# A sequential graph layer on one core: the recurrence in program order, its prepared work as tasks in the gaps

## The chip, the core and the metric

The kernel runs on one core of a Trainium2 chip. A core has TensorE (PE: matrix products, with a separate weight load, PEld), VectorE (DVE), ScalarE (ACT), GpSimd (POOL) and SyncE (SP, which here only issues DMA transfers). PE writes its products to PSUM, from which DVE and ACT read; the other data lie in SBUF. Time is the device time of one execution in microseconds; the time before is the median of 3 runs.

## The reference, cut to what matters

Four graph layers over 16 samples of 1024 nodes with 256 features, each of the form x = x + layer(relu(layernorm(x)), adj), all in float32. Layers 0 (attention), 1 (normalised adjacency) and 3 (two-layer network on neighbour sums) treat all nodes at once. Layer 2 is sequential: node i reads the new values of the nodes before it and the old values of the others.

```python
norm_adjT = jnp.swapaxes(adj, 1, 2) * dinv[:, :, None]

def step(h, i):
    x = jnp.take(h_e, i, axis=1)
    row = jnp.take(norm_adjT, i, axis=1)
    x_par = jnp.einsum('bj,bjd->bd', row, h)
    iou = x @ W_ioux.T + b_ioux + x_par @ W_iouh.T + b_iouh
    r, z = jnp.split(iou, 2, axis=1)
    r, z = (jax.nn.sigmoid(r), jax.nn.sigmoid(z))
    hc = jnp.tanh(x @ W_coux.T + b_coux + x_par * r @ W_couh.T + b_couh)
    h_new = z * x_par + (1.0 - z) * hc
    h = jax.lax.dynamic_update_slice(h, h_new[:, None, :], (0, i, 0))
    return (h, None)
h_out, _ = jax.lax.scan(step, h_e, jnp.arange(n))
```

## The kernel before

`layers_0_1()`, `layer_2()` and `layer_3()` run one after the other. In layer 2 the 1024 nodes are cut into 8 blocks of 128 (index t), and each block into 8 sub-blocks of 16 nodes (index s). 16 samples times 16 nodes make 256 rows, held as two groups (g) of 128 rows. The neighbour sum of a node has these parts:

- **base**: all blocks other than the one just before, with old or finished values; prepared one block ahead, as tasks (`base_tasks`);
- **last block**: the block just before; done between two blocks (`last_block`);
- **far** and **near**: sub-blocks of the same block that are done; near serves the next sub-block at once, far the later ones (`far_tasks`);
- inside the sub-block itself: the rounds. Three rounds (K = 3) always run. Each takes the change of h from the round before, spreads it over the adjacency inside the sub-block (`change`), and brings the gates up to date (`round_`). Where the chain of dependent nodes in a sub-block has more than three links, further rounds run (`one_more`), under a branch on a value that the kernel worked out from the data.

```python
def last_block(t, bxt, dv):
    for b0 in range(0, B, 4):
        hr = big.tile([P, 4, D], F32, name="hr")
        nc.sync.dma_start(hr, hn_d[b0 : b0 + 4, (t - 1) * P : t * P].rearrange("b p d -> p b d"))
        ao = big.tile([P, 4, P], F32, name="ao")
        nc.sync.dma_start(ao, a["adj"][b0 : b0 + 4, (t - 1) * P : t * P, t * P : (t + 1) * P] ...)
        nc.gpsimd.tensor_tensor(ao, ao, dv[:, b0 : b0 + 4], ALU.mult)
        for b in range(4):
            pb = psum.tile([P, DC, P], F32, name="pb")
            for c in range(DC):
                nc.tensor.matmul(pb[:, c], hr[:, b, c * P : (c + 1) * P], ao[:, b], start=True, stop=True)
            nc.vector.tensor_add(bxt[:, :, b0 + b], bxt[:, :, b0 + b], pb)

# gate_tasks(he, s): r (two tasks) and z with c (two tasks) of the inputs of sub-block s,
# wx products into PSUM tiles "pf", moved to gr (ACT) and gz (DVE)

def change(dh, x, ai):
    px = psum.tile([P, DC, G2 * GR], F32, name="px")
    ...                                     # px = dh x ai: 4 products of 128 columns
    for g in range(G2):
        add(pxr[:, g], aig[g], dh[:, g])    # the same sum with rows and columns swapped, kept in PSUM
    dx = work.tile([P, DC, G2 * GR], F32, name="dx", bufs=1)
    nc.vector.tensor_copy(dx[:, 0], px[:, 0])
    nc.scalar.activation(dx[:, 1], px[:, 1], AF.Copy)
    for c in range(DC):
        nc.vector.tensor_add(x[:, c], x[:, c], px[:, c])
    return dx

def round_(dx, x, rx, h, fill, to):
    ...                                     # pr += wh x dx: 4 products of 256 columns
    for e in range(DC):
        nc.scalar.activation(r[:, e], pr[:, e], AF.Sigmoid)
        nc.vector.tensor_mul(r[:, e], r[:, e], x[:, e])
        if rx is not None:
            nc.vector.tensor_sub(drx[:, e], r[:, e], rx[:, e])
    ...                                     # pz += dx x wh: 4 products of 256 columns
    nc.scalar.activation(z, pz, AF.Sigmoid)
    nc.scalar.activation(w, pz, AF.Sigmoid, scale=-1.0)
    fill()
    ...                                     # pc += drx x wh: 4 products of 256 columns
    nc.vector.tensor_mul(z, z, pxr)
    if h is not None:
        nc.vector.tensor_sub(z, z, h)
    fill()
    for g in range(G2):
        nc.scalar.activation(hc[:, g], pc[:, g], AF.Tanh)
        nc.vector.tensor_mul(w[:, g], w[:, g], hc[:, g])
        nc.vector.tensor_add(to[:, g], z[:, g], w[:, g])
    return r
```

The main loop, cut. The framework orders the instructions of each engine by itself, from the program and its own estimate of when each can start; `fill()` only says where in the program a share of the tasks stands.

```python
for t in range(NT):
    ...                                     # loads and base_tasks of block t + 1
    for s in range(NS):
        x = ...                             # bxt + near
        seed(x, *gx)                        # gates of the inputs into pr, pz, pc; x transposed into pxr
        ...                                 # gate_tasks of the next sub-block join the others
        fill()
        rx = round_(x, x, None, None, fill, ho)
        for k in range(1, K):
            dx = change(dh, x, ai)
            fill()
            ...                             # round_ again, with fill
        with tc.If(n_more[0][s] > 0, preferred_fallthrough_block=False):
            one_more(x, rx, h, ho, ai)      # no fill inside
            with tc.If(n_more[1][s] > 0, preferred_fallthrough_block=False):
                with tc.For_i(0, n_more[1][s], 1):
                    one_more(x, rx, h, ho, ai)
        for g in range(G2):
            nc.sync.dma_start(hn_d[g * GB : (g + 1) * GB, j0 : j0 + S], h[:, g])
        ...                                 # near products, far_tasks
    if t + 1 < NT:
        last_block(t + 1, bxt_next, dv_next)
```

Of the kernel before, what the change touches and what calls it, by code (L numbers as in the profile page):

```python
# [16 lines left out]
P = 128  # L17
# [9 lines left out]
K = 3  # L27
# [11 lines left out]
def gnn_stack(ctx: ExitStack, tc: tile.TileContext, a: dict, out: bass.AP):  # L39
# [273 lines left out]

    def layer_2():
        with ExitStack() as st:
# [28 lines left out]
            def levels():  # L344

                with ExitStack() as once:
# [14 lines left out]
                    pt = psum.tile([P, 2 * D], F32, name="pf", bufs=2)  # L361
# [16 lines left out]
            def base_tasks(t, bxt, dv):  # L378
# [4 lines left out]
                def load(b):  # L383
                    ab = big.tile([P, NT, P], F32, name="ab")
                    nc.sync.dma_start(ab, rows(a["adj"][b])[:, :, t * P : (t + 1) * P])
                    nc.gpsimd.affine_select(out=ab[:, t], in_=ab[:, t], compare_op=ALU.is_ge, fill=0.0, base=0,
                                            pattern=[[-1, P]], channel_multiplier=1)
                    hb = big.tile([P, NT, D], F32, name="hb")
                    if t > 1:
                        nc.sync.dma_start(hb[:, : t - 1], rows(hn_d[b])[:, : t - 1])  # L390
                    nc.sync.dma_start(hb[:, t:], rows(he_d[b])[:, t:])
                    loaded[b] = ab, hb

                def task(b, k, held):
                    def run():
                        if k == 0:
                            if b == 0:
                                load(0)
                            if b + 1 < B:
                                load(b + 1)  # L400
                            held.append(psum.tile([P, DC, P], F32, name="pb"))
# [3 lines left out]
                        for c, j in todo:  # L405
                            nc.tensor.matmul(pb[:, c], hb[:, j, c * P : (c + 1) * P], ab[:, j],  # L406
                                             start=j == jts[0], stop=j == jts[-1])
                        if k == len(jts) - 1:
                            nc.vector.tensor_mul(bxt[:, :, b], pb, dv[:, b][:, None].to_broadcast([P, DC, P]))
                            del loaded[b]  # L410
                    return run
# [8 lines left out]
            def last_block(t, bxt, dv):  # L420

                for b0 in range(0, B, 4):
                    hr = big.tile([P, 4, D], F32, name="hr")
                    nc.sync.dma_start(hr, hn_d[b0 : b0 + 4, (t - 1) * P : t * P].rearrange("b p d -> p b d"))
                    ao = big.tile([P, 4, P], F32, name="ao")
                    nc.sync.dma_start(ao, a["adj"][b0 : b0 + 4, (t - 1) * P : t * P, t * P : (t + 1) * P]
                                      .rearrange("b p i -> p b i"))
                    nc.gpsimd.tensor_tensor(ao, ao, dv[:, b0 : b0 + 4], ALU.mult)
                    for b in range(4):
                        pb = psum.tile([P, DC, P], F32, name="pb")  # L430
                        for c in range(DC):
                            nc.tensor.matmul(pb[:, c], hr[:, b, c * P : (c + 1) * P], ao[:, b], start=True, stop=True)
                        nc.vector.tensor_add(bxt[:, :, b0 + b], bxt[:, :, b0 + b], pb)

            def load_block(t):
# [7 lines left out]
                dp = big.tile([P, G2, P], F32, name="dp")  # L443
                for g in range(G2):
                    nc.sync.dma_start(dp[:, g], dinv_d[g * GB : (g + 1) * GB, t * P : (t + 1) * P][:, None]
                                      .to_broadcast([GB, S, P]))
                return he, dv, dp

            def load_sub(t, s, dp):


                j0 = t * P + s * S
                rem = P - s * S
                aj = big.tile([P, G2, P], F32, name="aj")
                for g in range(G2):
                    nc.sync.dma_start(aj[:, g, :rem], bass.AP(
                        tensor=a["adj"].tensor, offset=a["adj"].offset + g * GB * N * N + j0 * N + j0,
                        ap=[[N * N, GB], [N, S], [1, rem]]))
                nc.gpsimd.tensor_tensor(aj[:, :, :rem], aj[:, :, :rem], dp[:, :, s * S :], ALU.mult)
                ai = big.tile([P, G2, GB, S], F32, name="ai")  # L460
                for g in range(G2):
                    nc.gpsimd.tensor_tensor(ai[:, g], aj[:, g, :S][:, None].to_broadcast([P, GB, S]), before, ALU.mult)
                bd = None
                if s < NS - 1:
                    bd = big.tile([P, G2, GB, P - S], F32, name="bd")
                    for g in range(G2):
                        nc.gpsimd.tensor_tensor(
                            bd[:, g, :, : rem - S], aj[:, g, S:rem][:, None].to_broadcast([P, GB, rem - S]),
                            own[:, :, None].to_broadcast([P, GB, rem - S]), ALU.mult)
                return ai, bd  # L470

            def gate_tasks(he, s):


                hs = big.tile([P, DC, G2 * GR], F32, name="hs")
                for c in range(DC):
                    nc.gpsimd.tensor_copy(hs[:, c].rearrange("p (b i) -> p b i", b=B), he[:, c, :, s * S : (s + 1) * S])
                gr = big.tile([P, DC, G2 * GR], F32, name="gr")
                gz = big.tile([P, G2, 2 * D], F32, name="gz")

                def task_r(e):
                    def run():
                        pg = psum.tile([P, 2 * D], F32, name="pf", bufs=2)
                        for c in range(DC):
                            nc.tensor.matmul(pg[:, : G2 * GR], wx[:, c, e * P : (e + 1) * P],
                                             hs[:, c], start=c == 0, stop=c == DC - 1)
                        nc.scalar.activation(gr[:, e], pg[:, : G2 * GR], AF.Identity, bias=br[:, e : e + 1])
                    return run

                def task_z(g):  # L490
                    def run():
                        pg = psum.tile([P, 2 * D], F32, name="pf", bufs=2)
                        for c in range(DC):
                            nc.tensor.matmul(pg, hs[:, c, g * GR : (g + 1) * GR], wx[:, c, D:],
                                             start=c == 0, stop=c == DC - 1)
                        nc.vector.tensor_add(gz[:, g], pg, bzc)
                    return run
                return (gr, gz), deque([task_r(0), task_r(1), task_z(0), task_z(1)])

            def far_tasks(bxt, h, bd, s):  # L500

                far = P - (s + 2) * S

                def task(g, c, b4):
                    def run():
                        pf = psum.tile([P, 4, P - 2 * S], F32, name="pf", bufs=2)
                        nc.tensor.matmul(pf[:, :, :far], h[:, g, c * P : (c + 1) * P], bd[:, g, b4 : b4 + 4, S : S + far],
                                         start=True, stop=True)
                        to = bxt[:, c, g * GB + b4 : g * GB + b4 + 4, P - far :]
                        nc.vector.tensor_add(to, to, pf[:, :, :far])  # L510
                    return run
                if far <= 0:
                    return deque()
                return deque(task(g, c, b4) for g in range(G2) for c in range(DC) for b4 in (0, 4))
# [5 lines left out]
            pxr = psum.tile([P, G2, D], F32, name="pxr")  # L520
# [6 lines left out]
            def seed(base, gr, gz):  # L527

                nc.scalar.activation(pr, gr, AF.Copy)
                for g in range(G2):  # L530
                    for c in range(DC):
                        nc.tensor.matmul(pxr[:, g, c * P : (c + 1) * P], base[:, c, g * GR : (g + 1) * GR], ident,
                                         is_transpose=True, start=g == 0 and c == 0, stop=True, skip_group_check=True)
                nc.vector.tensor_copy(pz, gz[:, :, :D])
                nc.scalar.activation(pc, gz[:, :, D:], AF.Copy)

            def change(dh, x, ai):

                px = psum.tile([P, DC, G2 * GR], F32, name="px")
                aig = [ai[:, g].rearrange("p b i -> p (b i)") for g in range(G2)]  # L540
                for g in range(G2):
                    for c in range(DC):
                        nc.tensor.matmul(px[:, c, g * GR : (g + 1) * GR], dh[:, g, c * P : (c + 1) * P], aig[g],
                                         start=g == 0 and c == 0, stop=True, skip_group_check=True)
                for g in range(G2):
                    add(pxr[:, g], aig[g], dh[:, g])
# [7 lines left out]
            def round_(dx, x, rx, h, fill, to):  # L554


                for e in range(DC):
                    for c in range(DC):
                        add(pr[:, e], wh[:, c, e * P : (e + 1) * P], dx[:, c])
                r = work.tile([P, DC, G2 * GR], F32, name="r")  # L560
# [8 lines left out]
                for g in range(G2):  # L569
                    for c in range(DC):  # L570
                        add(pz[:, g], dx[:, c, g * GR : (g + 1) * GR], wh[:, c, D : 2 * D])
# [4 lines left out]
                fill()  # L576
# [3 lines left out]
                nc.vector.tensor_mul(z, z, pxr)  # L580
# [4 lines left out]
                for g in range(G2):  # L585
                    nc.scalar.activation(hc[:, g], pc[:, g], AF.Tanh)  # L586
                    nc.vector.tensor_mul(w[:, g], w[:, g], hc[:, g])  # L587
                    nc.vector.tensor_add(to[:, g], z[:, g], w[:, g])
                return r
# [292 lines left out]
```

## Time and profile before

| what | before |
|---|---|
| time, median of 3 runs | 5858.35 us (5854.73 to 5863.71) |
| span of the profiled execution | 5861.5 us |
| PE busy | 5334.5 us (91%) |
| DVE busy | 2630.8 us (45%) |
| ACT busy | 1398.0 us (24%) |
| POOL busy | 1348.0 us (23%) |
| mean granted clock of TensorE | 0.959 |
| recurrence of layer 2, from the first copy into x to the last store of h | about 1500 to 4397 us |

Busy shares are averages over layers with different limits, so the part that the change touches has to be read in windows. A window's row has its ends, its length, then the busy time (and instructions) of PE, PEld, DVE, ACT and POOL, the granted clock, the busy share of the DMA engines and GB/s. In a list in order of time each row has start, length, engine, line, operation and tiles; in square brackets stands how long the engine had been idle before it and what released it.

### The profile page before, as it was taken

What the parts mean: (1) busy time and instruction counts of PE and PEld (TensorE: products, weight loads), DVE (VectorE), ACT (ScalarE), POOL (GpSimd) and SP (SyncE); (2) the same over time, 40 slices, a digit from 0 to 9 for tenths busy, and PEclk for the clock granted to TensorE, in tenths of its full rate; (3) what the DMA queues carried; (4) which work ended last, traced back from release to release, by engine and by line L of the source; (5) the groups of instructions that cost most, each with busy time, mean ns of one, the idle gap of its engine ahead of it and who ended that gap; (6) DMA issues with size and microseconds to landing.
All of it is one profiled execution on the core that took longest, in us unless ns stands there. A gap on an engine that the chain in (4) does not pass through costs nothing. (4 is left out here: it accounts for less than half of the span.)

```text
span 5861.5 us, 61829 instructions
## 1 busy us (share of the span) xinstructions
PE 5334.5 (91%) x22527; PEld 3683.7 (63%) x22527; DVE 2630.8 (45%) x6353; ACT 1398.0 (24%) x2970; POOL 1348.0 (23%) x1653
## 2 busy tenths in 40 slices
PE   6999999994898998989889899898887999999999
PEld 3545545553787776767768778776664555555565
DVE  3444444431354554545545455454554433434433
ACT  1122121110122221222222222222322322323222
POOL 2222222221111111111111111111103433433422
PEclk9999999997998998989989999898998999999999
DMA  3323223217433223322123332321004221221210
GB/s 122 115 110 113 94 87 115 108 46 211 145 98 93 87 64 103 92 76 86 60 79 106 98 93 90 103 67 47 8 10 180 73 101 57 95 94 58 101 51 15
DMA packets 478248, 519.82 MB, mean 89 GB/s; under 512 B 31232, under 2 KB 429824, under 8 KB 475648
## 3 DMA queue, kind: packets, MB, share of 16 engines
q1 hardware_dynamic: 461952, 447.41, 23.9%
q0 software_dynamic: 15872, 67.18, 3.0%
q8 instruction: 214, 3.51, 0.2%
q14 instruction: 210, 1.72, 0.1%
HBM read 430.58 MB, written 83.95 MB: 88 GB/s over the span
## 5 line engine op out<-in xcount | busy, mean ns | idle before, releaser
L406 PE MATMUL pb<-ab,hb 128*128 128x128 f32 x3648 | 525.9, 284 | 61.8 <-DMA hb<-he_d 36.4
L406 PEld LDWEIGHTS pb<-ab,hb 128*128 128x128 f32 x3648 | 506.8, 199 | 104.0 <-issue 44.2
L756 PE MATMUL ph<-ag,w 128*128 128x512 f32 x1024 | 481.3, 613 | 34.0 <-DVE hh L760 33.9
L152 PE MATMUL pa<-at,h 128*128 128x512 f32 x1024 | 457.5, 601 | 34.8 <-DVE ag L157 34.8
L741 PE MATMUL pa<-at,h 128*128 128x512 f32 x1024 | 455.5, 596 | 31.7 <-DMA at<-in_adjT 31.7
L152 PE MATMUL pa<-at,q 128*128 128x512 f32 x1024 | 448.4, 594 | 0.0
L794 PE MATMUL po<-w,hh 128*128 128x256 f32 x2048 | 447.7, 379 | 0.0
L794 PEld LDWEIGHTS po<-w,hh 128*128 128x128 f32 x2048 | 387.8, 190 | 59.3 <-issue 7.9
L566 DVE TENSOR_TENSOR r<-r,x 128x256 f32<-128x256 f32 x450 | 174.8, 430 | 446.6 <-ACT r L565 446.6
L756 PEld LDWEIGHTS ph<-ag,w 128*128 128x128 f32 x1024 | 179.3, 190 | 296.0 <-DVE hh L760 151.6
L152 PEld LDWEIGHTS pa<-at,h 128*128 128x128 f32 x1024 | 194.2, 192 | 271.4 <-issue 223.4
L741 PEld LDWEIGHTS pa<-at,h 128*128 128x128 f32 x1024 | 194.2, 191 | 264.3 <-issue 262.0
L565 ACT ACTIVATE r<-pr 128x256 f32<-128x256 f32 x450 | 148.6, 382 | 838.1 <-PE pr L525 838.1
L152 PEld LDWEIGHTS pa<-at,q 128*128 128x128 f32 x1024 | 191.1, 190 | 237.6 <-issue 237.6
L762 POOL TENSOR_TENSOR ss<-ss,sq 128x512 f32<-128x512 f32 x224 | 305.1, 1362 | 117.6 <-ACT sq L759 113.0
L525 PE MATMUL pc<-wh,drx 128*128 128x256 f32 x1288 | 310.7, 383 | 10.4 <-DVE drx L568 10.4
L525 PE MATMUL pr<-dx,wh 128*128 128x256 f32 x1288 | 315.4, 383 | 0.0
L525 PE MATMUL pz<-wh,dx 128*128 128x256 f32 x1288 | 310.6, 380 | 0.0
L587 DVE TENSOR_TENSOR w<-w,hc 128x256 f32<-128x256 f32 x450 | 190.6, 459 | 267.1 <-ACT hc L586 267.1
L525 PEld LDWEIGHTS pc<-wh,drx 128*128 128x128 f32 x1288 | 237.0, 190 | 79.5 <-DVE drx L568 29.4
L525 PEld LDWEIGHTS pr<-dx,wh 128*128 128x128 f32 x1288 | 242.2, 193 | 43.2 <-issue 3.3
L525 PEld LDWEIGHTS pz<-wh,dx 128*128 128x128 f32 x1288 | 245.4, 190 | 33.6
(170 smaller groups left out, 8213.8 us busy)
## 6 DMA issues: line engine op xcount, KB each, us to landing
at<-in_adjT SPq DMA_DIRECT2D x128, 1024.0 KB
ab<-in_adj SPq DMA_DIRECT2D x128, 512.0 KB
x<-in_x SPq DMA_DIRECT2D x16, 1024.0 KB
x_d<-x POOLq DMA_DIRECT2D x16, 1024.0 KB, 7.9
he_d<-h POOLq DMA_DIRECT2D x16, 1024.0 KB, 6.3
heT_d<-hT POOLq DMA_DIRECT2D x16, 1024.0 KB, 4.2
he<-heT_d SPq DMA_DIRECT2D x16, 1024.0 KB
hb<-he_d SPq DMA_DIRECT2D x16, 1024.0 KB
```

The costliest lines, as they stand in the source:

```text
L152: nc.tensor.matmul(pa, h[:, mt, c * P : (c + 1) * P], at[:, mt, n0 : n0 + 512], start=mt == 0, stop=mt == NT - 1)
L406: nc.tensor.matmul(pb[:, c], hb[:, j, c * P : (c + 1) * P], ab[:, j], start=j == jts[0], stop=j == jts[-1])
L525: nc.tensor.matmul(to, lhsT, rhs, start=False, stop=True, skip_group_check=True)
L565: nc.scalar.activation(r[:, e], pr[:, e], AF.Sigmoid)
L566: nc.vector.tensor_mul(r[:, e], r[:, e], x[:, e])
L587: nc.vector.tensor_mul(w[:, g], w[:, g], hc[:, g])
L741: nc.tensor.matmul(pa, h[b][:, mt, c * P : (c + 1) * P], at[b][:, mt, n0 : n0 + NH], start=mt == 0, stop=mt == NT - 1)
L756: nc.tensor.matmul(ph, w1[:, c, k * P : (k + 1) * P], ag[:, c, n0 : n0 + NH], start=c == 0, stop=c == DC - 1)
L762: nc.gpsimd.tensor_tensor(ss, ss, sq, ALU.add)
L794: nc.tensor.matmul(po, hh[:, c, k * P : (k + 1) * P], w2[:, c], start=c == 0, stop=c == HC - 1)
```

## The change

All of it is in layer 2. The four computing engines now take their instructions in program order (`manual_schedule`), and the program says by hand where each task of prepared work stands: `fill(weight)` puts a share of the tasks, by estimated cost, into each gap of the chain on PE, and the moves of their results out of PSUM are kept in a list `late` and issued by `evict()` behind the chain's own work. Further:

- The last block's products are tasks in the first sub-block of the next block (`last_tasks`). Its first 16 nodes can't wait for them, so each sub-block also adds its part for those 16 (`next_block`, into the PSUM tile pnx).
- pxr, which kept x with rows and columns swapped by accumulating, is gone; each round transposes x anew (xr).
- The input gates of the next sub-block are worked out behind the rounds: in the gaps of the first extra round where there is one, in the else branch where there is none.
- PSUM: pb, px and the pf of two buffers give way to pf of three buffers for all tasks, one tile pa for px, xr and near, and pnx.
- h is stored by GpSimd's DMA queue instead of SyncE's.

```diff
-            def last_block(t, bxt, dv):
...
+            def last_tasks(t, bxt, dv):
+                n = P - S
...
+                        pl = psum.tile([P, DC, n], F32, name="pf", bufs=3)
+                        for c in range(DC):
+                            nc.tensor.matmul(pl[:, c], hr[:, b - b0, c * P : (c + 1) * P], ao[:, b - b0],
+                                             start=True, stop=True)
+                        to = bxt[:, :, b, S:]
+                        return lambda: nc.vector.tensor_add(to, to, pl)
+                    return 0.4, run
+                return [task(b) for b in range(B)]
...
+            def next_block(h, bd, n, start):
                 for c in range(DC):
+                    for g in range(G2):
+                        nc.tensor.matmul(pnx[:, c, g * GR : (g + 1) * GR], h[:, g, c * P : (c + 1) * P],
+                                         bd[:, g, :, n : n + S], start=start and c == 0 and g == 0, stop=True,
+                                         skip_group_check=True)
...
-            pxr = psum.tile([P, G2, D], F32, name="pxr")
+            pnx = psum.tile([P, DC, G2 * GR], F32, name="pnx")
...
+            late = []
+            def evict():
+                while late:
+                    late.pop(0)()
...                                                      # in change
-                for g in range(G2):
-                    add(pxr[:, g], aig[g], dh[:, g])
+                fill()
...                                                      # in round_, behind pr
+                xr = psum.tile([P, G2, D], F32, name="pa")
+                for g in range(G2):
+                    for c in range(DC):
+                        nc.tensor.transpose(xr[:, g, c * P : (c + 1) * P], x[:, c, g * GR : (g + 1) * GR], ident)
+                for g in range(G2):
+                    for c in range(DC):
+                        add(pz[:, g], dx[:, c, g * GR : (g + 1) * GR], wh[:, c, D : 2 * D])
+                evict()
...                                                      # further down in round_
-                fill()                                   # the one ahead of pc
...
-                nc.vector.tensor_mul(z, z, pxr)
+                nc.vector.tensor_mul(z, z, xr)
...                                                      # at the end of round_
+                evict()
...
-            def one_more(x, rx, h, ho, ai):
+            def one_more(x, rx, h, ho, ai, tasks=()):
+                tasks = list(tasks)
+                def fill():
+                    if tasks:
+                        late.append(tasks.pop(0)())
+                fill()
...
+            with tc.manual_schedule(engines={mybir.EngineType.PE, mybir.EngineType.DVE, mybir.EngineType.Activation, mybir.EngineType.Pool}):
...
+                        share = [base_todo.popleft() for _ in range(-(-len(base_todo) // (NS - s)))]
+                        todo, lists = [], [behind, share]
...
+                        def fill(weight):
+                            nonlocal spent, part
+                            part += weight
+                            while todo and (part > 0.999 or spent + 0.5 * todo[0][0] < part * total):
+                                cost, task = todo.pop(0)
+                                spent += cost
+                                late.append(task() or (lambda: None))
+                        x = work.tile([P, DC, G2 * GR], F32, name="x")
+                        fill(0.15)
...
+                        rx = round_(x, x, None, None, lambda: fill(0.2), ho)
...
+                            dx = change(dh, x, sub.ai, lambda: fill(0.12))
...
+                                rx = round_(dx, x, rx, ho, lambda: fill(0.2), dh)
...
+                                rx = round_(dx, x, rx, None, lambda: fill(1.0), h)
+                        with tc.If(n_more[0][s] > 0, preferred_fallthrough_block=False) as more_or_not:
+                            one_more(x, rx, h, ho, sub.ai, gx.tasks if gx else ())
...
+                        if gx:
+                            with more_or_not.Else():
+                                for task in gx.tasks:
+                                    late.append(task())
+                                    if len(late) > 1:
+                                        late.pop(0)()
+                                evict()
+                            gx.seed_r()
...
-                        nc.sync.dma_start(hn_d[g * GB : (g + 1) * GB, j0 : j0 + S], h[:, g])
+                            nc.gpsimd.dma_start(hn_d[g * GB : (g + 1) * GB, j0 : j0 + S], h[:, g])
...
+                        elif t + 1 < NT:
+                            next_block(h, sub.bd, 0, False)
+                            near = pnx
+                            behind = last_tasks(t + 1, bxt_next, dv_next)
```

## The prediction

> **What bounds the kernel now.** I read the page's slices first, then the work by line, then the stage that changes in windows and in order of time. The chain that ended last is of no use here: it covers only layer 3, which is not touched. The slices say that TensorE is the busy engine nearly everywhere:
>
> ```profile
> PE   6999999994898998989889899898887999999999
> DVE  3444444431354554545545455454554433434433
> PEclk9999999997998998989989999898998999999999
> ```
>
> From slice 10 to slice 30 (layer 2) the 9 turns into a mix of 8 and 9 and the granted clock dips with it. Layer 2 is the only layer that the change edits; its recurrence runs from 1500 us (first copy into x) to 4397 us, 2897 us. Cut at the starts of the eight blocks of 128 nodes, the windows (engines in the order PE, PEld, DVE, ACT, POOL, then clock and DMA share) read:
>
> ```profile
> 2240.00:2620.00 380.00, 341.75 (x1776) 282.93 (x1776) 189.76 (x443) 94.80 (x227) 62.44 (x92) 0.94 0.30 86
> 3047.00:3372.00 325.00, 302.21 (x1593) 251.68 (x1594) 161.35 (x379) 80.87 (x192) 54.97 (x83) 0.95 0.34 101
> 4099.00:4397.00 298.00, 257.66 (x1193) 203.41 (x1192) 160.37 (x392) 88.42 (x214) 34.83 (x50) 0.98 0.04 10
> ```
>
> PE is busy 90% in a block; no other engine passes 54%, DMA about 0.3. The missing clock and much of the missing 10% lie at the seven boundaries between blocks, where the next block needs the outputs of the one just ended:
>
> ```profile
> 2204.50:2242.00 37.50, 21.58 (x70) 15.47 (x68) 9.80 (x23) 1.12 (x2) 5.52 (x8) 0.60 0.47 131
> 2583.50:2620.00 36.50, 20.91 (x68) 15.20 (x66) 8.93 (x21) 0.21 (x1) 5.06 (x6) 0.55 0.51 137
> 3335.90:3371.50 35.60, 22.82 (x73) 15.68 (x72) 8.90 (x20) 1.59 (x3) 6.21 (x9) 0.63 0.59 161
> ```
>
> All seven sum to 256.1 us. The clock in them is 0.55 to 0.63, and the order of time shows why they are long:
>
> ```profile
> 2592.35 1.20 PE L432 MATMUL pb<-ao,hr 128*128 128x128 f32 x4 [7.38 <-DMA hr<-hn_d]
> 2593.58 0.42 DVE L433 TENSOR_TENSOR bxt<-bxt,pb 128x256 f32<-128x256 f32 x1 [7.12 <-PE pb L432]
> 2594.05 0.93 PEld L432 LDWEIGHTS pb<-ao,hr 128*128 128x128 f32 x4 [0.81 <-DVE bxt L433]
> ```
>
> First a round trip through memory (7.38 us without a matmul), then sixteen turns of 1.74 us in which PE and DVE pass one PSUM buffer to and fro. Nothing else runs. The second loss is in the extra rounds, which run only in sub-blocks with a long dependency chain and have nothing to fill their gaps:
>
> ```profile
> 2573.81 1.13 PE L543 MATMUL px<-ai,dh 128*128 128x128 f32 x8 [0.15 <-DVE dh L594]
> 2574.78 1.03 PE L525 MATMUL pxr<-dh,ai 128*128 128x256 f32 x4
> 2579.57 1.99 PE L525 MATMUL pc<-wh,drx 128*128 128x256 f32 x8 [0.31 <-DVE drx L568]
> ```
>
> The h of this sub-block ends at 2572.87 and that of its extra round at 2583.86: 11.0 us. L594 runs 33 times, so there are 33 extra rounds.
>
> [...] before, PE sat 0.56 us idle when it passed an untaken extra round ("PEq L665" at 3337.49 us), so I use 0.5 us for each way in or out.
>
> **The work on PE, before and after.** Eight matmuls of 256 columns follow each other in 1.70 us, so one takes 0.213 us at full clock, one of 128 columns 0.107, one of 512 0.427; three transposes took 0.43 us, 0.14 each. Counts come from the groups by shape. Before: gate products 5400 x 0.213 = 1152; px 1288 x 0.107 = 137; pxr 644 x 0.213 = 137 and 256 x 0.14 = 36; base 3138 x 0.107 = 335; input gates 496 x (0.427 + 0.213) = 318; far products, 1344 columns x 128 = 143; near 448 x 0.107 = 48; last block 48. Sum 2354 us, of 2897.
>
> After: pxr's accumulation (173 with its transposes) becomes four transposes of x in each of 225 rounds, 225 x 4 x 0.14 = 126. The last block drops from 128 to 112 columns, 42. New are the products for the next block's first 16 columns (next_block), 56 x 8 x 0.107 = 48. Sum 2349 us. So **the change does not lessen the work**; it can gain only what PE loses now, 543 us, of which clock and idling are both part.
>
> **Boundaries.** 256 us go as a stage. Their matmuls become tasks in the first sub-block of the next block and I charge them there. The round trip stays: h to hr took 8.4 us (h ends 2583.9, first product 2592.35). In the new order PE has, after h, the rest of the input gates (5.1), next_block (0.86) and a branch, about 6.8 us, before the first last-block task; it then stands in front of that task in program order. The loads of later pairs (two buffers) may hold it again. I charge 6 us for each boundary: 256 - 42 = 214 gained. Some 2 us of slow clock after each boundary go too: 14.
>
> **Extra rounds.** The first extra round of a sub-block gets the four input-gate tasks (0.85, 0.85, 1.7, 1.7 us) in its gaps instead of after it. From the branch: 0.5 + 0.85 + px 0.85 + 1.05 (copies to dx) + 5.6 (pr, transposes, pz, pc) + 1.7 + 1.7 + 1.0 for the branches = 13.3, less the 5.6 that gates and branch cost without it: 7.7 us. A second extra round has no tasks: 10.3. With 26 first (the waits on L667 number 26) and 7 later: 200 + 72 = 272 against 33 x 10.8 = 356. Gained: 84.
>
> **Ordinary sub-blocks.** In the block from 3047 us, without extra rounds, h ends 36.2 us apart on average (3081.7 to 3335.4, seven steps). Work before, at full clock: 15.36 for three rounds, 3.42 px and pxr, 0.56 transposes, 5.98 base, 5.05 gates, 0.86 near, 2.55 far = 33.8; lost 2.4. After: 15.36 + 1.68 + 1.71 + 5.98 + 5.05 + 0.86 + 2.55 + 0.75 last + 0.86 next = 34.8. What must be filled is the chain's own gaps: 1.07 us to build x, 1.05 twice from px to dx, 1.5 to 1.7 twice from pc to h (tanh 0.38, DVE 2 x 0.38, hand-overs), 6.3 in all; the tasks on hand are 10 us, dealt by weights 0.15, 0.2, 0.12, 0.2, 0.12 and the rest, so each gap gets about what it needs (0.2 x 10 = 2.0 against 1.7). The rest of the lost time is the branch (1 us) and hand-overs: I put 1.6. So 36.4, and 56 x 0.2 = 11 us worse. In block 8 no base tasks exist; its chain alone is 31.5 us by the same steps, against 31 now: nothing gained.
>
> **Sum.** 214 + 14 + 84 - 11 = 301, and I take off 18 for waits on the three pf buffers where far and last-block tasks crowd (one is held by the base sum for seven tasks, so a fourth task waits for an eviction that stands behind the chain on DVE). 5858 - 283 = **5575 us**.
>
> **Rivals.** (a) *Head-of-line waits*: in program order one late operand (hr, a mask on GpSimd that waits for ab, a full pf) stops the chain, where the old order could run something else. For it: GpSimd now waits in order for ab (591.7 us of such waits before) and also issues the h stores. Against: masks are asked for one sample ahead, some 14 us, and DMA share is 0.3. At 2 us more for each of 64 sub-blocks: 5700. (b) *The gaps were already full*: if PE's lost 2.4 us are hand-overs that remain and extra rounds save nothing, only boundaries count: 5858 - 228 + 11 = 5641. (c) *The new order packs better*: if ordinary sub-blocks come down to their work plus 0.5, 35.3, then 56 x 1.1 = 62 more, and without the 18: 5495. (d) *The branch costs more with an Else*: 2 us instead of 1 for 63 sub-blocks adds 63: 5638.
>
> **Range and chances.** (c) sets the low end, 5480; (a) or (d) with some of (b) the high end, 5690. A gain below 2% (5741) needs rival (a) at 2.6 us in every sub-block, or 24 us more of stall at each boundary; possible, not likely. Faster 0.90, same 0.06, slower 0.04.
>
> **What would show it.** In the profile after: no stage near 36 us without activations between blocks, clock in layer 2 at 0.98 or more against 0.94, PE's busy share there 95% or more; the first product of hr waiting under 4 us on its load; sub-blocks without extra rounds 35 to 37 us apart, about 8 us more with one; layers 0, 1 and 3 unchanged. The prediction is wrong if PE shows waits on pf evictions or on hr of tens of us, if the recurrence before layer 3 is longer than 2680 us, or if the weights leave gaps that the dx and h chains show as PE idle time.

## The result and the profile after

The changed kernel takes 5643.65 us (median of 4 runs, 5635.94 to 5647.66) against 5857.64 us: ratio 0.9632, 95% interval 0.9615 to 0.9648, 214 us less. The prediction was 5575 us, 283 us less, with a range of 5480 to 5690.

The slices of the page after:

```profile
PE   6999999995799998999889999998869999999999
DVE  3454444532254555555545455555544343343433
PEclk9999999997899999999999999999989999999999
```

At this coarse scale the dips of the clock inside layer 2 are gone. The recurrence runs from 1500 to 4181 us, 2681 us instead of 2893 to the last store; the layers around it take as long as before. Its whole stretch as one window, before (first row) and after (second row; columns as before):

```profile
1500.00:4397.00 2897.00, 2608.17 (x13382) 2153.41 (x13381) 1442.90 (x3401) 736.50 (x1762) 451.87 (x680) 0.95 0.27 78
1500.00:4181.00 2681.00, 2493.04 (x13844) 2107.12 (x13844) 1450.09 (x3435) 732.74 (x1764) 533.70 (x866) 0.98 0.29 85
```

PE's busy time falls by 115 us although it does no less, at a clock of 0.98 instead of 0.95, and its idle time falls from 289 to 188 us. After the change, in windows cut at the starts of blocks 3, 5 and 8:

```profile
2165.00:2507.00 342.00, 323.39 (x1836) 275.46 (x1836) 187.30 (x446) 93.87 (x227) 69.83 (x114) 0.99 0.33 95
2901.00:3207.00 306.00, 289.43 (x1656) 247.77 (x1656) 158.97 (x376) 81.03 (x192) 63.70 (x104) 0.98 0.37 107
3872.00:4183.00 311.00, 262.34 (x1272) 207.20 (x1272) 174.43 (x414) 89.15 (x216) 58.44 (x89) 0.98 0.08 22
```

PE is busy 94.6% in the two whole blocks, where it was 90 to 93%, at a clock of 0.98 to 0.99. But the starts of the blocks still stand out:

```profile
2503.00:2523.00 20.00, 12.74 (x59) 10.76 (x58) 5.15 (x11) 2.35 (x5) 7.37 (x9) 0.74 0.42 131
3202.00:3222.00 20.00, 12.75 (x50) 9.80 (x49) 4.03 (x9) 1.87 (x5) 7.37 (x9) 0.74 0.53 159
```

PE is busy less than 13 of 20 us, at a clock of 0.74. In order of time, the boundary at 2897 us (the 26-us stage of turns is gone, the wait ahead of it is not). For the names: hr and ao are h and adjacency of the last block, hb and ab those of the base products, aj is adjacency as loaded, from which GpSimd makes bd for near, far and next_block; gz holds the z and c gates of the inputs; SPq, DVEq and the like are rows of an engine's sequencer: here issues of transfers, waits and branches.

```profile
2896.88 0.42 DVE L647 TENSOR_TENSOR h<-z,w 128x256 f32<-128x256 f32 x1
...
2899.56 1.23 POOL L766 DMA_DIRECT2D hn_d<-h  x2 [5.60 <-DVEq L752]
...
2902.52 0.88 SPq L441 DMA_DIRECT2D hr<-hn_d  x2
...
2905.34 1.17 PE L456 MATMUL pf<-ao,hr 128*128 128x112 f32 x4 [4.86 <-DMA hr<-hn_d]
...
2908.94 1.22 PE L414 MATMUL pf<-ab,hb 128*128 128x128 f32 x4 [2.44 <-DMA hb<-hn_d]
...
2912.49 2.42 PE L586 MATMUL pr<-x,wh 128*128 128x256 f32 x8
...
2924.94 0.67 PE L456 MATMUL pf<-ao,hr 128*128 128x112 f32 x4 [2.13 <-DMA hr<-hn_d]
...
2934.24 0.70 PE L456 MATMUL pf<-ao,hr 128*128 128x112 f32 x4 [1.21 <-DVE bxt L459]
```

x is ready at 2902.22 (DVE, 0.75 us from 2901.47), yet the first product of the chain (pr) starts at 2912.49: it stands in the program behind a last-block task that waits for hr and a base task that waits for hb, and the clock was 0.50 from 2905 to 2913 us. And the store of h leaves 2.3 us after h: GpSimd stands at the branch's join (DVEq L752), where the two ways meet again. Where the sub-block had no extra round it leaves later still, 3.7 us (first half, shown) and 5.3 us (second half) after h at 3200.73, released by DVE's moves of the gates:

```profile
3204.42 0.64 POOL L766 DMA_DIRECT2D hn_d<-h  x1 [10.04 <-DVE gz L538]
```

In the list of waits of the recurrence (engine and tile, what it waited for, us in total, times, longest) this row is PE's largest:

```profile
PE pf L456 <- DMA hr<-hn_d: 44.9, 14, 4.9
```

An extra round at 2886 us shows the gates (L528, L536) in its gaps; before, nothing stood there:

```profile
2885.60 1.03 PE L528 MATMUL pf<-hs,wx 128*128 128x256 f32 x4
...
2887.43 1.13 PE L599 MATMUL pa<-ai,dh 128*128 128x128 f32 x8 [0.80 <-DVE dh L662]
...
2888.39 1.03 PE L528 MATMUL pf<-hs,wx 128*128 128x256 f32 x4
...
2893.15 1.89 PE L586 MATMUL pc<-wh,drx 128*128 128x256 f32 x8
...
2894.88 3.60 PE L536 MATMUL pf<-wx,hs 128*128 128x512 f32 x8
```

PE waits 0.80 us once, for dh, and 5.1 us of gate work is done by the end.

To compare sub-blocks I took the time from one sub-block's last h to the next one's, 64 intervals for each kernel, and fitted them by least squares on the position s in the block, an extra round, later extra rounds, and an extra round in the sub-block before (which has already done the gates of this one), with terms of their own for the first sub-block of all and for block 8, which has no base tasks. "Net" is what a first extra round adds to its own sub-block and to the next. In us:

| kernel | s = 0, t > 0 | mean of s = 1 to 7 | first extra, net | each later extra |
|---|---|---|---|---|
| before | 69.1 | 36.2 | 11.2 + 0.6 = 11.8 | 11.6 |
| changed | 53.2 | 36.3 | 11.3 - 3.9 = 7.4 | 13.3 |

The seven intervals over a boundary together went from 515.0 to 388.3 us, all others (the first sub-block of all among them) from 2377.2 to 2291.0: 127 and 86 us make the gain.

### The profile page after: what moved, and what is told of

Read it like the earlier page. It is cut to its first block, busy times and chain, and to the rows that moved or that the text cites. A ratio compares the mean times of both kernels' runs of the same rounds, so it can differ in the third digit from the quotient of the medians.

```text
span 5644.6 us, 63144 instructions
## 1 busy us (share of the span) xinstructions
PE 5215.2 (92%) x22975; PEld 3637.5 (64%) x22975; DVE 2638.4 (47%) x6386; ACT 1393.6 (25%) x2970; POOL 1418.8 (25%) x1823
## 5 line engine op out<-in xcount | busy, mean ns | idle before, releaser
L414 PE MATMUL pf<-ab,hb 128*128 128x128 f32 x3648 | 517.7, 284 | 46.7 <-DMA hb<-he_d 34.4
L414 PEld LDWEIGHTS pf<-ab,hb 128*128 128x128 f32 x3648 | 492.2, 199 | 80.9 <-issue 41.1
L629 DVE TENSOR_TENSOR r<-r,x 128x256 f32<-128x256 f32 x450 | 187.3, 428 | 336.6 <-ACT r L628 336.6
L744 POOL TENSOR_TENSOR ho<-ho,dh 128x512 f32<-128x512 f32 x64 | 81.2, 1269 | 940.0 <-DVE dh L647 785.0
L157 DVE COPY ag<-pa 128x512 f32<-128x512 f32 x64 | 44.2, 690 | 488.0 <-PE pa L152 488.0
```

The source lines that it names most:

```text
L744: nc.gpsimd.tensor_tensor(ho, ho, dh, ALU.add)
```

## The experiments

All start from the changed kernel unless said otherwise. Times are medians; ratios are to the kernel before, which ran at 5855 to 5861 us beside them.

**Nothing ahead of the first round** at a boundary:

```diff
+                        clear = s == 0 and t > 0
-                        fill(0.15)
+                        if not clear:
+                            fill(0.15)
...                      # weights 0.2 and 0.12 become 0.25 and 0.17 where clear
```

> No task stands ahead of the first round of a block's first sub-block (t > 0, s = 0); its tasks go into the later gaps (weights 0, 0.25, 0.17, 0.25, 0.17, rest). Theory A (at a boundary the first last-block task waits in program order for hr and hb, and the chain behind it stands still): the first round starts at once, the waits of some 4.3 us for hr and 2 us for hb and the half clock after them are hidden, 7 to 9 us for each of 7 boundaries, 50 to 60 us: about 5590 us. Theory B (the first sub-block simply carries more work than the others, and PE's stall is made up later): the same work crowds into fewer gaps, at most 15 us gained: 5630 or more.

5621.29 us, ratio 0.9596 (0.9583 to 0.9609): 22 us gained, between the two theories. The boundary in order of time:

```profile
3194.55 0.89 SPq L441 DMA_DIRECT2D hr<-hn_d  x2
...
3195.02 1.97 PE L586 MATMUL pr<-x,wh 128*128 128x256 f32 x8 [1.07 <-DVE x L723]
...
3200.89 0.59 PE L456 MATMUL pf<-ao,hr 128*128 128x112 f32 x4
...
3209.36 0.67 PE L456 MATMUL pf<-ao,hr 128*128 128x112 f32 x4 [1.01 <-DMA hr<-hn_d]
```

The chain starts as soon as x is there and the first last-block product waits for nothing. So the wait was head-of-line (one late operand held all that stands behind it), as theory A said; but the same 16 tasks are now crowded and meet the next limit, the later pairs of hr (last line). A first sub-block came down from 53.2 to 48.9 us only.

**Four buffers for hr and ao**, loads three pairs ahead, on top of that:

```diff
-                    ao = big.tile([P, 2, n], F32, name="ao")
+                    ao = big.tile([P, 2, n], F32, name="ao", bufs=4)
...                      # hr likewise; load(2) and load(4) at the start, then load(b + 6)
```

> As the run with the first round clear of tasks, and four buffers instead of two for hr and ao, loads three pairs ahead. Theory A2 (what is left of the boundary, 48.9 us for the first sub-block against some 43 by its work, is PE waiting for the next pair of hr, which finds both buffers taken): 3 to 5 us for each boundary, 20 to 35 us: 5585 to 5600. Rival B2 (the waits for evictions of the three pf buffers hold it): 5615 to 5625.

5586.58 us, ratio 0.9536 (0.9523 to 0.9549): as theory A2 said. The first sub-block takes 44.3 us; waits for hr no longer show among PE's. The pf evictions were not what held it.

**The store inside the branch**, so that it needn't wait for the join:

```diff
+                            store()                  # last in the taken part
-                        if gx:
-                            with more_or_not.Else():
+                        with more_or_not.Else():
+                            store()                  # first in the else part
+                            if gx:
...                      # the stores behind the join go
```

> The stores of h stand inside the branch: first thing in the else part, last thing in the taken part, instead of behind the join of both. Theory A: in the three boundaries without an extra round the first store leaves 3.7 us earlier and the second 5.3 us, hr's wait of 3.9 us goes nearly, hb's wait shrinks; the four with an extra round keep theirs: 10 to 20 us gained, about 5630. Theory B: nothing, 5640 to 5650, because the wait moves to hb or to the next pair of hr.

5687.48 us, ratio 0.9704 (0.9687 to 0.9721): 44 us **slower**, which neither theory had. The store did leave at once; the load of hr did not:

```profile
3225.89 0.64 POOL L754 DMA_DIRECT2D hn_d<-h  x1 [5.86 <-DVE h L647]
...
3234.70 1.29 SPq L488 DMA_DIRECT2D aj<-in_adj  x2
3236.17 0.87 SPq L441 DMA_DIRECT2D hr<-hn_d  x2
...
3241.15 1.17 PE L456 MATMUL pf<-ao,hr 128*128 128x112 f32 x4 [8.73 <-DMA hr<-hn_d]
```

SyncE's issue of hr (3236.17) came behind that of aj (3234.70), and in front of aj it was standing until GpSimd's bd gave the buffer free at 3234.68; such waits for bd sum to 108.9 us in this run's recurrence, in the changed kernel's to 14.2 us. In the changed kernel hr comes ahead of aj (2902.52 against 2906.97 us). SyncE is still ordered by the framework, from its estimates, and an edit on another engine turned its order round.

**SyncE in program order too**, on top of that: the set of engines of `manual_schedule` gets SyncE.

> As the run with the stores inside the branch, with SyncE's queue in program order too. There the store left at once, yet SyncE issued hr 10 us later, behind the next sub-block's aj load, which waited for GpSimd to finish bd; in program order hr's load stands ahead of that aj load. Theory J (only SyncE's order spoilt that run): 5620 to 5635, 10 to 20 us better than the changed kernel. Rival K (program order on SyncE lets a load that waits for its buffer hold the others): 5660 or more.

5675.86 us, ratio 0.9691 (0.9676 to 0.9707): rival K, still 32 us slower than the changed kernel. hr is in time now, and the next load in the queue takes its place:

```profile
3236.59 0.67 PE L456 MATMUL pf<-ao,hr 128*128 128x112 f32 x4 [0.56 <-issue]
...
3241.39 1.19 PE L414 MATMUL pf<-ab,hb 128*128 128x128 f32 x4 [4.13 <-DMA hb<-hn_d]
```

Not all of the loss lies at the boundaries: the first sub-block of all takes 49.0 us, in the changed kernel 29.4, since its first base task waits for a load:

```profile
1514.67 2.04 PE L414 MATMUL pf<-ab,hb 128*128 128x128 f32 x8 [20.64 <-DMA hb<-he_d]
```

**Stores by SyncE**, as before the change:

```diff
-                            nc.gpsimd.dma_start(hn_d[...], h[:, g])
+                            nc.sync.dma_start(hn_d[...], h[:, g])
```

> The changed kernel with the stores of h issued by SyncE again, as before the change, not by GpSimd. Theory L (GpSimd stands at the join of the branch until DVE has moved the last gates, SyncE needs only h): the round trip is 3 to 5 us shorter where no extra round runs, 10 to 25 us in all: 5620 to 5635. Rival M (SyncE passes the same join, or its own queue is held by the wait for h): 5640 to 5660.

5697.3 us, ratio 0.9730 (0.9717 to 0.9744): 54 us slower, more than either theory had. SyncE too issued the store only 3.3 us after h (h ends at 3229.32):

```profile
3226.53 2.00 DVE L647 TENSOR_TENSOR h<-z,w 128x256 f32<-128x256 f32 x1
...
3232.59 2.25 SPq L766 DMA_DIRECT2D hn_d<-h  x2
```

And bd comes late, so late that it falls beside the chain (GpSimd's waits for pnx ahead of bd, a row that the changed kernel hasn't). I take it that loads waited behind the store; that is an inference, not shown:

```profile
POOL bd L508 <- PE pnx L551: 155.9, 24, 7.3
```

The move of DVE shown took 2.00 us, where all 194 that write h take 0.42 or 0.43 us in the changed kernel. In this run 49 of the 450 moves out of z and w took over 0.47 us, every one beside an instruction of GpSimd (25 beside bd), and none of the 375 with GpSimd idle did. That GpSimd causes it is seen in time only, not tried; how the 54 us divide between the late bd and the slow moves is not told apart.

**The framework's order** of the four engines, same program:

```diff
-            with tc.manual_schedule(engines={...PE, DVE, Activation, Pool}):
+            with ExitStack():
```

> The same program, but the framework orders the four engines again (no manual schedule). Theory C (the gain came from what the program does: no stage between blocks, gates in the gaps of extra rounds): within 40 us of the changed kernel, 5610 to 5690, since ordinary sub-blocks took 36.2 us before and 36.1 after. Theory D (the gain came from program order): most of the 214 us is lost, 5750 to 5860.

5592.95 us, ratio 0.9540 (0.9526 to 0.9555): theory C, and 51 us **faster** than program order, past the range of C. At the boundary the framework moved chain work ahead of the waiting task (the transposes of round 1 stand before the first hr product):

```profile
3188.80 0.38 PE L618 MATMUL pa<-ident,x 128*128 128x128 f32 x2
...
3190.72 0.70 PE L456 MATMUL pf<-ao,hr 128*128 128x112 f32 x4 [1.53 <-DMA hr<-hn_d]
```

Its first two sub-blocks take 42.1 and 44.3 us, by hand 53.2 and 38.8; the others agree within 0.7 us at each position. So it gained at the boundary and gave a part back in the sub-block behind it. With four buffers besides:

> The framework's order of the four engines with four buffers for hr and ao. Theory A2 (pairs of hr hold PE in any order): the first two sub-blocks, 42.1 and 44.3 us with the framework's order and two buffers, come down by 2 to 4 us for each boundary, 5565 to 5580. Rival N (the framework has put those tasks where their loads have landed): 5585 to 5600, no change.

5575.29 us, ratio 0.9507 (0.9493 to 0.9521): a gain of 18 us, theory A2; the two sub-blocks take 41.3 and 41.1 us.

**Gates as ordinary tasks** in the gaps, none in the extra round, no else part:

```diff
+                                    todo[:0] = zip((0.85, 0.85, 1.7, 1.7), gx.tasks)
+                                    total += 5.1
-                            one_more(x, rx, h, ho, sub.ai, gx.tasks if gx else ())
+                            one_more(x, rx, h, ho, sub.ai)
```

> The input gates of the next sub-block are ordinary tasks in the gaps of the third round's stretch, for every sub-block; the extra round has none and there is no else part. Theory E (extra rounds gained because the gates fill them): each first extra round costs 11 to 12 us again instead of 7.4 net, 29 of them, 119 us lost; the sub-blocks late in a block, which are bound by the chain and do the gates one after the other behind it, gain 2.5 us, some 55 us in all: 5690 to 5720. Rival F (gates in the branch bring nothing over tasks): 5600 to 5660.

5755.5 us, ratio 0.9828 (0.9813 to 0.9843): 112 us slower. Theory E in its first half, and past its range: a first extra round costs 12.7 - 1.8 = 10.9 us net, 3.5 more for each of 29. Its second half fell: late sub-blocks gained nothing (35.4 at s = 5 against 35.3), so the chain with the gates behind it did not bind them in the way I had put it.

**The stage back**, all sixteen last-block tasks behind next_block and none left for the first sub-block:

```diff
-                            behind = last_tasks(t + 1, bxt_next, dv_next)
+                            for _, task in last_tasks(t + 1, bxt_next, dv_next):
+                                late.append(task())
+                                if len(late) > 1:
+                                    late.pop(0)()
+                            evict()
+                            behind = []
```

> The last block's products are a stage between blocks again (all sixteen tasks one after the other behind next_block, none left for the first sub-block); everything else as changed. Theory G (the three parts of the change add up: no stage is worth what is left of the 214 us when the gates in the branch bring 112 and the hand-made order costs 51, so some 150 us): 5760 to 5800. Rival H (a stage with three PSUM buffers and program order is already short, some 22 us instead of 36): 5690 to 5740.

5707.07 us, ratio 0.9749 (0.9732 to 0.9766): 63 us slower, rival H. The first sub-block with its stage takes 62.3 us; before the change it was 69.1. So a part of the boundary's gain is not the missing stage but a shorter one.

**The z gates first** in the else part, on top of the clear first round and the four buffers:

```diff
-                                for task in gx.tasks:
+                                for task in gx.tasks[2:] + gx.tasks[:2]:
```

> As the run with the first round clear and four buffers, and in the else part the gates of z and c come ahead of those of r. Theory O (in every sub-block without an extra round the near products wait 0.56 to 0.84 us at the branch's end for DVE to move the last z gates; with the r gates last, which ACT moves, DVE is done earlier): 0.5 to 0.8 us in each of some 35 sub-blocks, 17 to 28 us: 5558 to 5570. Rival P (the wait is on the join itself, or ACT's moves and its copy into pr take DVE's place): 5580 to 5595.

5551.54 us, ratio 0.9472 (0.9459 to 0.9485): 35 us gained, more than theory O, and the fastest version. In the list of waits of the run without this edit (engine and tile, what it waited for, us in total, times, longest) these two rows are PE's for the near products; with the edit the first stays and the second is gone:

```profile
PE pa L776 <- DVEq L756: 20.5, 22, 0.9
...
PE pa L776 <- DVE gz L540: 16.5, 30, 0.6
```

Nearly every sub-block behind one without an extra round, where the else part has run, came down by 0.83 us; those behind an extra round mostly stayed as they were. Over 34 such sub-blocks that is 28 us, the upper end of theory O; the first sub-blocks of blocks gained somewhat more (44.3 to 42.4 us). The row accounts for 0.55 (16.5 by 30) of the 0.83; the rest is not told apart (DVE is also free earlier to build x).

**That version in the framework's order:**

> The best version so far (first round clear, four buffers, z gates first) with the four engines in the framework's order. Theory Q (order by hand lost its 51 us at the boundary alone, where the framework moved the chain past the waiting tasks; with the boundary mended by hand both orders are worth the same): 5540 to 5565. Rival R (the framework's order is the better one throughout): 5500 to 5530. Rival S (with good positions in the program, order by hand wins): 5575 or more.

5591.18 us, ratio 0.9548 (0.9535 to 0.9561): rival S. With the tasks in good places program order is 40 us faster; with the places of the change it was 51 us slower. In the framework's order the clear first round and the z gates in front made it 16 us slower (5575.29 to 5591.18), so the best of each order are 24 us apart, not 40.

## Why the prediction was right, and where it was short

- **What bounds, and that work isn't lessened**: right. PE's matmuls grow from 22527 to 22975, exactly the 448 of next_block; the 900 transposes equal the 644 + 256 they replaced. The gain is idle time and clock (0.95 to 0.98), in about equal parts.
- **Extra rounds**: right in mechanism, and in size for the first of a sub-block: 7.7 predicted, 7.4 measured, and taking the gates out of them costs 112 us. Their count was off: 29 first and 4 later, not 26 and 7 (the waits on L667 that I counted miss some). A later one costs 13.3, not 10.3, more than the 11.6 before; why is not shown. Together 29 x 4.4 - 4 x 1.7 = 121 us, where I had 84.
- **Ordinary sub-blocks**: 36.4 predicted, with 0.75 of last-block work that in fact lies in the first sub-block, so 35.65; measured 36.1 at s = 1 to 7 of the block without extra rounds (36.2 before). Over the 50 such sub-blocks of blocks 1 to 7 (the first of all, which gained 7 us, among them) that is 26 us worse than I had.
- **Block 8**: 31.5 predicted, and the mean of its four sub-blocks without extra rounds is 31.7, but that agreement is luck: three of them follow an extra round, which has done their gates, and take 30.8 us; the one that doesn't takes 34.4 (32.1 before). By the fit block 8 is 21 us slower than before; I had no change.
- **Boundaries**: the step that failed in size is "*I charge 6 us for each boundary*", resting on "*in the new order PE has, after h, the rest of the input gates (5.1), next_block (0.86) and a branch, about 6.8 us, before the first last-block task*". By my terms a first sub-block should take 69.1 - 36.6 (stage) + 6 (stall) - 2 (clock) + 5.3 (7 x 0.75, last-block work that I had put into the other sub-blocks) + 0.2 (as every sub-block) = 42.0 us. It takes 53.2, 11.2 more. In the list above PE idles 4.86 us for hr, 2.44 for hb, 2.13 for the next pair and 1.21 for a pf tile, and then twice 0.5 to 0.6 for ao, 11.8 us in all (9.2 to 11.8 over the seven boundaries), and the half clock, which I had thought gone with the stage, costs some 2.6 more by estimate (5.2 us of busy PE at 0.50): 14.4 us where I charged 6. The other 2.8 us are not told apart. With the first round clear and four buffers the sub-block takes 44.3 us; PE still idles there, 5.7 us in block 5, about what I had charged, though for pnx, x, hb and an eviction and not for hr.
- **Why 6.8 us of work did not cover the round trip**: the order of time shows that the store of h stands behind the same branch. Without an extra round it leaves only when the gates are moved; with one, the gates are already done and cover nothing. From h to the first hr product it is 8.0 us at 2897 and 9.9 us at 3201, where I took 8.4. What an earlier store alone is worth stays open, since the runs that moved it changed the order of the loads as well.
- **The 18 us for pf**: about right. PE's waits for evictions of pf tiles sum to 14.0 us in the recurrence, 10.3 of them at last-block tiles, so they are part of the boundaries' excess.
- **The sum**: against my terms, boundaries are 78 us worse, ordinary sub-blocks 26, block 8 21, and extra rounds 37 better: 301 - 78 - 26 - 21 + 37 = 213 us, eviction waits included, and 214 is what was measured. That 5644 lies as near to 5575 as it does owes something to errors that offset each other.
- **Rivals**: (a) head-of-line waits came, but mostly at boundaries. Nothing at all was gained by program order as it stood; it cost 51 us. (b) fell with the extra rounds. (c) did not come: ordinary sub-blocks take 36.1, not 35.3. (d) came in part: z gates first takes 0.83 us off the end of the else part, 28 us in 34 sub-blocks, about the 26 that ordinary ones were short; that these are the same is argued, not shown. The parts of the gain, taken away one at a time, don't add up: gates 112, stage 63, order -51 give 124 of 214. About 48 more is the stage that became shorter by itself (7 times 69.1 - 62.3); some 42 stay unassigned.
- **The signs I named**: "*the first product of hr waiting under 4 us*" failed at four of seven boundaries (3.8 to 4.9), the recurrence is 2681 us, at the limit of 2680 that I had set, and waits on hr "*of tens of us*" came (44.9). All three pointed at the step that failed.

## What to carry to other kernels

A task that fills a gap must not stand ahead of the critical chain unless its operands have landed by then: where it waits for memory (here up to 4.9 us for hr), put the chain first and fetch more buffers ahead (22 and 35 us here), and check that the work meant to cover a round trip isn't what delays its start (here the store left 3.7 us after h). The order of the issues in SyncE's queue is a schedule of its own; the run with the earlier store was 44 us slower, and in it the load of hr came after a blocked one. Order by hand is worth as much as its places: the same engines gained or lost 40 to 51 us with it.

## What the runs showed of the hardware that was not expected

- **A join cost more than the branch** (0.56 us on PE before). Behind it, GpSimd's and SyncE's issues, which need only h, came 2.3 to 5.3 us after h; inside the branch GpSimd's came 0.3 us after the first half of it (3225.59 to 3225.89). With the gates so ordered that ACT, not DVE, moves the last of them, a sub-block behind the else part took 0.83 us less.
- **Half clock after short stalls.** The clock fell during the wait of 4.86 us (0.71 from 2902 to 2905) and was 0.50 from 2905 to 2913 us, in which 1.2 us of work and a second wait of 2.44 us lie; it was 0.94 in the 4 us after. At the boundary at 3201 us, waits of 3.90 and 2.79 us went with 0.62 from 3210 to 3212 and 0.50 from there to 3220. The wait of 2.13 us at 2924.94 left it at 1.00 (2924 to 2926). Before the change it was 0.50 from 2588 us, during the wait of 7.38 us, to 2624, and 0.90 in the 4 us after. In the 8 us from 2905, PE was busy for 5.2 us; four base products took 1.22 us there (2908.94) and 0.62 us at 2919.51. So I estimate that the stall cost 2.6 us more than its own length, half of the 5.2.
